# A four-layer graph network on one core: other PSUM banks and a thinned transfer queue at the head of a loop, and a pass that starts on rows that are already mixed

## The chip, the core and the metric

The kernel runs on one core of a Trainium2 chip. The core has five engines that run side by side, each with its own queue of instructions: TensorE (PE in the profile; its weight loads are listed as PEld), VectorE (DVE), ScalarE (ACT), GpSimd (POOL) and SyncE (SP). Here SP does little else than issue transfers (DMA); POOL issues the gathers (indirect transfers) and some small arithmetic. The engines meet only at semaphores. Working memory is SBUF, with 128 partitions; matmuls write to PSUM, eight banks of 512 fp32 numbers in each partition.

The metric is the device time of one execution in microseconds, as a median over runs. A profile is one further execution, with every instruction's start and length.

## What is computed

A graph of 2708 nodes with 128 features each, and a dense 2708 x 2708 adjacency `adj`, most of whose entries are zero. Four layers, each added to its input and normalized:

```python
x = layernorm(x + L0(x, adj))   # nearest-neighbour layer
x = layernorm(x + L1(x, adj))   # attention layer
x = layernorm(x + L2(x, adj))   # normalized adjacency
x = layernorm(x + L3(x, adj))   # adjacency, concatenation, relu

def L1(X, A, W, a):             # the layer that matters here
    XW = X @ W
    s_col, s_row = XW @ a[0, :128], XW @ a[0, 128:]
    den = exp(leaky_relu(s_row[:, None] + s_col[None, :], 0.01))
    num = A @ den
    att = where(num != 0, den / num, 0)
    return A @ (att @ XW)       # the last product is a pass over A
def L2(x, A, W, b):
    d = 1 / sqrt(A.sum(1) + 1e-6)
    return (d[:, None] * A * d[None, :] @ x) @ W.T + b
def L3(x, A, W, b):
    return relu(concat([x, A @ x]) @ W.T + b)
```

Everything is fp32.

## The kernel before

The adjacency comes transposed (`adjT`) and is too large to stay in SBUF: of its 22 row tiles (21 of 128 rows and one of 20) six stay in `res`, the others stream through a ring buffer, `ring`. A *pass* over the adjacency (`by_panels`, line 189) runs over six column chunks of at most 512; for each it sums 21 products of 128 rows, and for every third chunk the last 20 rows of three chunks. It makes a chunk's result in one PSUM bank (`acc`), which `into_hT` (line 231) copies out with ACT. Four panels of four row tiles each are loaded per chunk by SP (line 178), into the four slots of the ring. `by_panels` runs four times; its *third last* run is the last product of L1, `A @ (att @ XW)`, and the two after it belong to L2 and L3.

`att @ XW` is the *loop* (`block_layer`, line 1674). Nodes are sorted by score and taken in 44 blocks of 62, two blocks a step. Within a block, the sum `num` is known from running totals of the blocks before it (`carry`) and the adjacency rows of the block's own nodes. A step works on one half of the columns (HALF = 1354) and one pair of blocks q; 22 pairs by two halves give 44 steps. The 1354 columns are worked on as a *wide* piece of 1024 and a *narrow* one of 330. Step i does this:

- `load(i + 2)` (line 1119): two gathers on POOL (line 1123) bring the two blocks' adjacency rows into one of three strips of the ring, and two transfers on SP (line 1130) bring their two rows of running totals out of `carry`.
- `fetch_xw` (line 1102): POOL gathers a tile of XW rows, in the first steps.
- `find_num` (line 1683): TensorE makes `num` for the narrow piece of step i and for the wide piece of step i + 1 (line 1689).
- `add(i - 1)` (line 1708): TensorE adds the step before into `hacc` (line 1571), three banks.
- `find_inv` (line 1694): ACT makes 1/num by a logarithm and an exponential (lines 1546 and 1549).
- `mix_1`, `mix_2`, `mix_3` (lines 1556, 1560, 1563): DVE corrects and weighs it. The first of them reads `num` and makes `err`.
- `keep` (line 1697): SP stores rows of `err` as new running totals into `carry` (line 1704); usually four transfers a step.

All engines run the loop in the order in which the program writes it (`manual_schedule`); outside, a scheduler places the instructions. Tiles carry their own dependencies: whoever writes a tile or takes over its memory waits for those who used it.

The PSUM of the loop is one pool, `ops`: two buffers of two banks for the wide `num`, one bank for the narrow, three for `hacc`. Before the loop the same eight banks hold, in order, three `acc`, three `mis`, `places` and a count tile.

*Ahead of the loop* the running totals of every fourth block come from a product over the whole adjacency (`add_line`, line 1418), a row tile and a half of the columns at a time, into two `acc` banks, one for each half. `end_half(h)` (line 1435) copies such a bank to SBUF with ACT (lines 1440 and 1441), and `send_half` (line 1445) stores it in four transfers into the rows of `carry` from 96 on (line 1449): for the left half from ACT's queue, for the right half, with which TensorE ends, from SP's. Steps 0 to 21 use the left half of `carry`, steps 22 to 43 the right half. The last 20 rows of the adjacency, which the product over the adjacency needed in another arrangement, are loaded back in six transfers (line 1539). In SP's queue the scheduler puts three of these six earlier, among panel loads; the other three come last. The order there is: rows for steps 0 and 1, four stores, three reloads, the branch, rows for step 2.

*After the loop* its last `add` follows ten transposes (line 1755) of the left half's result, which ACT scales into `mixed` (line 1757), the weights of the pass that follows; `mixed` and `carry` are the same memory. Then `hacc` of the right half is copied to SBUF in three pieces (`evacuate`, lines 160 and 162). `two_layers` (line 1763) turns the other twelve tiles (line 1772), DVE scales them into `mixed` (line 1773), and the pass begins. `first` is the number of tiles mixed before, 10 (`EARLY`). For another distribution of the scores there is `dense_layer` in place of `block_layer`; it is not run here.

L253 with output `dinv` is a power on POOL for the layer after; L252 on DVE makes its input.

Of the kernel before, what the change touches and what calls it, by code (L numbers as in the profile page):

```python
# [52 lines left out]
def kernel(  # L53
# [132 lines left out]
        for g in range(1, GROUPS):  # L186
            (engine or nc.scalar.copy)(rows[few(g)], rows[few(0)])

    def by_panels(weights, done, tick=None, ready=(), first=None):

        ready = list(ready)
        accs = {}

        def product(c, i, src, w):
            lhsT = weights(i)[few(c) if i == FULL else slice(None)]
            start = c not in accs  # L200
            if start:
# [36 lines left out]
    def rows_of(y):  # L238
        return lambda i: y[:, i, :]
# [892 lines left out]
    with tc.tile_pool(name="rank", bufs=1) as rank:  # L1132
# [302 lines left out]
        def end_half(h):  # L1435

            if not carries:
                carries.append(big.tile([P, NQ * P], F32, tag="y", name="carry"))
            tot = heads[h]
            nc.scalar.copy(tot[:, : edges[4] - edges[3]], banks[h][:, : edges[4] - edges[3]])  # L1440
            nc.scalar.copy(tot[:64, edges[4] - edges[3] :], banks[h][:64, edges[4] - edges[3] : span])
            if h == 0:
                send_half(h, tot, nc.scalar)

        def send_half(h, tot, queue):

            for g in range(4):
                w = edges[g + 1] - edges[g]
                queue.dma_start(
                    carries[0][HEADS : HEADS + 2 * NCH, h * HALF + edges[g] : h * HALF + edges[g + 1]],  # L1450
                    tot[32 * g : 32 * g + 2 * NCH, :w],
                )
# [81 lines left out]
        xws, lw = work["xws"], work["lw"]  # L1534
        load(0)
        load(1)
        send_half(1, heads[1], nc.sync)
        for c in range(C):
            nc.sync.dma_start(res[few(c), FULL - S, cols[c]], adjT[FULL * P :, cols[c]])
        order.close()  # L1540
    more.close()

# [37 lines left out]
    mixed = carry.rearrange("p (t d) -> p t d", d=D)  # L1580
    EARLY = HALF // P
    over = nc.values_load(flag[0:1, 0:1], min_val=0, max_val=N)
    def dense_layer():


        nonlocal mis_pool, hT
        with (
# [6 lines left out]
            y2g = carry.rearrange("p (t d) -> p t d", d=D)  # L1594
            nc.sync.dma_start(y2g[:, :FULL, :], y2_rows[: FULL * P, :].rearrange("(t p) d -> p t d", p=P))
            nc.sync.dma_start(y2g[:LAST, FULL, :], y2_rows[FULL * P :, :])
            load_x(range(T))
            add_bias(b2_sb)

# [74 lines left out]
    def block_layer():  # L1674
        with (
            tc.tile_pool(name="own", bufs=2) as own,
            tc.tile_pool(name="ops", bufs=1, space=bass.MemoryType.PSUM) as ops,
        ):
            nc.scalar.preload_act_table_set("natural_log_exp_and_others")
            nums, invs, haccs = {}, {}, {}  # L1680
            pieces = {"wide": (0, WIDE, 2), "narrow": (WIDE, NARROW, 1)}

            def find_num(i, piece):
                q, (c0, w, bufs) = steps[i][1], pieces[piece]
# [11 lines left out]

            def keep(i, piece, err):

                (h, q), (c0, w, _) = steps[i], pieces[piece]
# [8 lines left out]
            def add(i):  # L1708
                h, q = steps[i]
                if q == 0:  # L1710
                    haccs[h] = ops.tile([P, 3 * CW], F32, tag="hacc", name="hacc")
                for piece, (c0, w, _) in pieces.items():
                    add_up(w, q, invs[i, piece], haccs[h][:, c0 : c0 + w])

            engines = {nc.tensor, nc.vector, nc.scalar, nc.sync, nc.gpsimd}
            with tc.manual_schedule(engines={e.engine for e in engines}):
# [3 lines left out]
                for i, (h, q) in enumerate(steps):  # L1720
                    if i + 2 < len(steps):
                        load(i + 2)
                    if late_q:
                        fetch_xw(xws, late_q.pop(0))
                    find_num(i, "narrow")
                    if i + 1 < len(steps):
                        find_num(i + 1, "wide")
# [8 lines left out]
                        nc.scalar.copy(mT[:, :HALF], haccs[0][:, :HALF])  # L1736
                    if i + 1 < len(steps):
                        errs = {}
                        for piece, (c0, w, _) in pieces.items():
# [4 lines left out]
                        for piece, (c0, w, _) in pieces.items():  # L1744
                            mix_3(w, q, invs[i, piece], h * HALF + c0)
                    else:
                        for piece, (c0, w, _) in pieces.items():
# [14 lines left out]

    def two_layers(arm, first):
        nonlocal acc_pool, mis_pool, hT
        acc_pool = arm.enter_context(tc.tile_pool(name="acc2", bufs=3, space=bass.MemoryType.PSUM))
        mis_pool = arm.enter_context(tc.tile_pool(name="mis2", bufs=5, space=bass.MemoryType.PSUM))

        hT = gb
        for t in range(first, T):
            p = pw[t]  # L1770
            pt = mis_tile()
            nc.tensor.transpose(pt[:p, :D], mT[:, t * P : t * P + p], ident)  # L1772
# [110 lines left out]
```

## Time and profile before

| what | us |
|---|---|
| median of 8 runs | 1039.68 |
| lowest and highest of them | 1036.59 and 1043.03 |
| the profiled execution | 1035.87 |
| its span in the trace | 1034.1 |
| head of the loop, first num matmul | 477.48 |
| the loop's last hacc matmuls end | 700.3 |
| third last pass, first product | 702.77 |

The profiled execution's mean granted clock of TensorE was 0.986. How the page goes on in time, in 40 slices of 25.9 us each; a digit is the busy share in tenths:

```profile
PE   0789999999999999798999999999999999999996
DVE  5886438999966578856999999992212121222222
ACT  0000126555611236405777776661101000020000
POOL 5000000000557763027665444410211000000000
DMA  9999340000167757696565455566675866575662
```

The run of nines in the right half of DVE's row is the loop: DVE is as full as TensorE there. After it come the three last passes, in which TensorE is full and the others mostly idle. In rows of the profile a group is given by its line and engine and by output and input (`num<-ring,lw`: from the ring and the block weights into `num`). An fp32 matmul stands in the trace as two records, so that x12 is six matmuls. SPq is SP's queue: the rows give the issuing of a transfer, not its landing.

### The profile page before, as it was taken

To read this page: it belongs to the slowest core of one execution; us is meant where nothing else is said; L and a number is where in the kernel's file an instruction comes from. 1 tells how busy PE (TensorE), PEld (TensorE's weight loads), DVE (VectorE), ACT (ScalarE), POOL (GpSimd) and SP (SyncE) were. 2 spreads that over 40 slices of the span, in tenths; PEclk is the share of its full clock that TensorE was granted. 3 is DMA by queue.
4 is the path that set the end of the run, shared out by engine and by line. 5 is a ranking of instruction groups with operands and counts; after the bars stand their busy time and mean duration, and the time that the engine had idled before them with its cause. 6 is when DMAs were issued, how large, how long until landed. Compare 5 with 4: busy or idle time off the path is not lost.

```text
span 1034.1 us, 11663 instructions
## 1 busy us (share of the span) xinstructions
PE 971.1 (94%) x3773; PEld 475.7 (46%) x3773; DVE 638.9 (62%) x1364; ACT 332.2 (32%) x609; POOL 261.5 (25%) x339
## 2 busy tenths in 40 slices
PE   0789999999999999798999999999999999999996
PEld 0346544444444557463333333344445444664444
DVE  5886438999966578856999999992212121222222
ACT  0000126555611236405777776661101000020000
POOL 5000000000557763027665444410211000000000
PEclk9899999999999999799999999999999999999998
DMA  9999340000167757696565455566675866575662
GB/s 323 374 370 315 90 160 1 0 1 1 44 218 234 234 160 253 253 399 196 147 168 148 131 150 154 137 204 208 193 224 154 289 202 215 144 261 179 205 185 62
DMA packets 101985, 191.00 MB, mean 185 GB/s; under 512 B 14006, under 2 KB 43326, under 8 KB 101914
## 3 DMA queue, kind: packets, MB, share of 16 engines
q1 hardware_dynamic: 83880, 152.34, 44.4%
q0 software_dynamic: 17728, 37.62, 13.3%
q8 instruction: 32, 0.52, 0.2%
q14 instruction: 39, 0.32, 0.1%
q10 hardware_dynamic: 306, 0.20, 0.1%
HBM read 214.80 MB, written 4.16 MB: 212 GB/s over the span
## 4 chain that ended last, share of the span: by engine, by line
PE 50%; DVE 1%; ACT 1%; DMA 0%; issue 0%; POOL 0%; POOLq 0%
PE acc L204 28%; PE hacc L1571 10%; PE num L1689 10%; PE mis L285 1%; PE mis L1818 0%; DMA ring<-carry 0%; ACT gb L234 0%; PE mis L1784 0%; DVE inv L1560 0%; PE mis L1814 0%; DVE inv L1563 0%; POOL rstd L253 0%; DVE err L1556 0%; PE mis L1772 0%; ACT m_rows L160 0%
## 5 line engine op out<-in xcount | busy, mean ns | idle before, releaser
L1123 POOL DMA_INDIRECT ring<-in_adjT,slot_i x88 | 92.9, 1056 | 95.4 <-PE num L1689 76.3
L1689 PE MATMUL num<-ring,lw 128*64 128x512 f32 (+1 forms) x528 | 111.5, 551 | 4.9 <-DMA ring<-carry 2.4
L1571 PE MATMUL hacc<-inv,xws 128*128 128x512 f32 (+1 forms) x264 | 111.7, 560 | 0.3 <-DVE inv L1563 0.3
L714 PE MATMUL acc<-zT,z 128*128 128x512 f32 (+2 forms) x252 | 102.2, 552 | 0.0
L1546 ACT ACTIVATE inv<-num,plain 128x1024 f32<-128x1024 f32 x88 | 80.6, 916 | 57.9 <-PE num L1689 43.6
L253 POOL TENSOR_TENSOR rstd<-rstd,minus_half 128x4 f32<-128x4 f32 (+1 forms) x18 | 17.3, 959 | 311.8 <-DVE rstd L252 311.8
L234 ACT COPY gb<-acc 128x512 f32<-128x512 f32 (+2 forms) x18 | 9.6, 534 | 249.4 <-PE acc L204 249.4
L715 ACT COPY key<-acc 128x512 f32<-128x512 f32 (+2 forms) x126 | 67.1, 534 | 55.1 <-PE acc L714 27.7
L1571 PEld LDWEIGHTS hacc<-inv,xws 128*128 128x128 f32 x264 | 46.6, 190 | 77.1 <-issue 32.8
L204 PE MATMUL acc<-ring,y 128*128 128x512 f32 (+2 forms) x192 | 80.4, 547 | 0.5 <-issue 0.5
L1556 DVE TENSOR_TENSOR err<-inv,num 128x1024 f32<-128x1024 f32 x88 | 74.6, 853 | 9.0 <-ACT inv L1549 6.9
L759 POOL DMA_INDIRECT got<-y_rows,where x66 | 71.2, 1079 | 30.1 <-DVE near_sum L772 10.2
L1563 DVE SCALAR_TENSOR_TENSOR inv<-gb,g_inv,inv 128x1024 f32<-128x1024 f32 x88 | 77.0, 912 | 0.1
L204 PE MATMUL acc<-ring,xs 128*128 128x512 f32 (+2 forms) x192 | 76.7, 543 | 0.0
L204 PE MATMUL acc<-ring,carry 128*128 128x512 f32 (+2 forms) x192 | 74.5, 542 | 0.0
L204 PE MATMUL acc<-ring,m_rows 128*128 128x512 f32 (+2 forms) x192 | 74.3, 542 | 0.0
L1560 DVE SCALAR_TENSOR_TENSOR inv<-err,inv 128x1024 f32<-128x1024 f32 x88 | 72.5, 861 | 0.1
L714 PEld LDWEIGHTS acc<-zT,z 128*128 128x128 f32 x252 | 45.9, 190 | 50.3 <-issue 44.9
L1549 ACT ACTIVATE inv<-inv 128x1024 f32<-128x1024 f32 x88 | 67.6, 768 | 2.8
L584 POOL TENSOR_TENSOR slot_e<-near,sim 128x44 f32<-128x44 f32 (+2 forms) x3 | 0.7, 238 | 253.9 <-DVE near L581 253.8
L1689 PEld LDWEIGHTS num<-ring,lw 128*64 128x64 f32 x528 | 35.8, 136 | 62.6 <-issue 47.6
L718 DVE MAX8 near<-key 128x8 f32<-128x2708 f32 x21 | 62.3, 2965 | 2.7 <-ACT key L715 2.7
(379 smaller groups left out, 1355.4 us busy)
## 6 DMA issues: line engine op xcount, KB each, us to landing
ring<-in_adjT SPq DMA_DIRECT2D x74, 1024.0 KB
ring<-in_adjT SPq DMA_DIRECT2D x20, 677.0 KB
ring<-in_adjT SPq DMA_DIRECT2D x17, 768.0 KB
part<-in_adjT SPq DMA_DIRECT2D x12, 1024.0 KB
ring<-in_adjT SPq DMA_DIRECT2D x17, 552.0 KB
more<-in_adjT SPq DMA_DIRECT2D x10, 677.0 KB
res<-in_adjT SPq DMA_DIRECT2D x4, 1280.0 KB
part<-in_adjT SPq DMA_DIRECT2D x3, 768.0 KB
```

The costliest lines, as they stand in the source:

```text
L204: nc.tensor.matmul(accs[c][: lhsT.shape[-1], :w], lhsT=lhsT, rhs=src, start=start, stop=stop)
L714: nc.tensor.matmul(pks[c][:p, : cw[c]], lhsT=z2[:, :p], rhs=zT[:, cs], start=False, stop=True)
L715: nc.scalar.copy(key[:p, cs], pks[c][:p, : cw[c]])
L759: nc.gpsimd.indirect_dma_start(out=got[:p, :], out_offset=None, in_=y2_rows[:, :], in_offset=bass.IndirectOffsetOnAxis(ap=where[:p, t, k : ...
L1123: nc.gpsimd.indirect_dma_start(out=rows[i][:KC, n, :], out_offset=None, in_=adj_half[:, :], in_offset=bass.IndirectOffsetOnAxis(ap=slot_i[ ...
L1546: nc.scalar.activation(inv, num[:, :w], AF.Ln, scale=plain[:, 0:1], bias=plain[:, 1:2])
L1549: nc.scalar.activation(inv, inv, AF.Exp, scale=-1.0)
L1556: nc.vector.tensor_mul(err, inv, num[:, :w])
L1560: nc.vector.scalar_tensor_tensor(inv, err, 2.0, inv, op0=ALU.subtract, op1=ALU.mult)
L1563: nc.vector.scalar_tensor_tensor(inv, gb[:, col : col + w], g_inv[:, q : q + 1], inv, op0=ALU.max, op1=ALU.mult)
L1571: nc.tensor.matmul(haccs[:, o:e], lhsT=xws[:, q, :], rhs=inv[:, o:e], start=(q == 0), stop=(q == NQ - 1))
L1689: nc.tensor.matmul(num[n * (BJ + 2) : (n + 1) * (BJ + 2), o:e], lhsT=lw[:, 2 * q + n, :], rhs=rows[i][:, n, c0 + o : c0 + e], start=True, ...
```

## The change

There are three edits.

1. In the loop, the wide `num` tiles of even and odd steps come from two pools of their own, the narrow one and `hacc` from two more. The pools are opened so that `hacc` has the banks of the three `acc` tiles, the narrow `num` that of the first `mis`, the odd steps those of the other two `mis`, and the even steps those of `places` and the count. The right half's two copies in `end_half` are made by DVE.
2. The four stores of the right half move into the loop, one in each of steps 4 to 7, and the six reloads of the last rows, one in each of steps 8 to 13. Each stands on SP behind the step's two row loads and ahead of its stores of `err`. (In the branch with `dense_layer` the reloads stand at its beginning.)
3. `by_panels` takes a function to call after a given number of products of the first chunk. The third last pass begins with eight products, then the twelve transposes and scalings come, then the rest. The two PSUM pools of the passes change places.

The diff without its renamings:

```diff
-    def by_panels(weights, done, tick=None, ready=(), first=None):
+    def by_panels(weights, done, tick=None, ready=(), first=None, between=(0, None)):
...
                 product(c, i, src, w)
+                if c == 0 and i + 1 == between[0]:
+                    between[1]()
...
             tot = heads[h]
-            nc.scalar.copy(tot[:, : edges[4] - edges[3]], banks[h][:, : edges[4] - edges[3]])
-            nc.scalar.copy(tot[:64, edges[4] - edges[3] :], banks[h][:64, edges[4] - edges[3] : span])
+            copy = nc.vector.tensor_copy if h else nc.scalar.copy
+            copy(tot[:, : edges[4] - edges[3]], banks[h][:, : edges[4] - edges[3]])
+            copy(tot[:64, edges[4] - edges[3] :], banks[h][:64, edges[4] - edges[3] : span])
...
-        def send_half(h, tot, queue):
+        def send_half(h, tot, queue, groups=range(4)):
-            for g in range(4):
+            for g in groups:
...
         load(0)
         load(1)
-        send_half(1, heads[1], nc.sync)
-        for c in range(C):
-            nc.sync.dma_start(res[few(c), FULL - S, cols[c]], adjT[FULL * P :, cols[c]])
+        right = heads[1]
...
+    def last_rows_back(chunks):
+        for c in chunks:
+            nc.sync.dma_start(res[few(c), FULL - S, cols[c]], adjT[FULL * P :, cols[c]])
...
-            tc.tile_pool(name="ops", bufs=1, space=bass.MemoryType.PSUM) as ops,
+            tc.tile_pool(name="hops", bufs=1, space=bass.MemoryType.PSUM) as hops,
+            tc.tile_pool(name="nops", bufs=1, space=bass.MemoryType.PSUM) as nops,
+            tc.tile_pool(name="odd", bufs=1, space=bass.MemoryType.PSUM) as odd,
+            tc.tile_pool(name="even", bufs=1, space=bass.MemoryType.PSUM) as even,
...
+            def num_tile(n, w, name):
+                pool = nops if w == NARROW else (even, odd)[n % 2]
+                return pool.tile([P, w], F32, tag=f"num{w}", name=name)
...
-                num = nums[i, piece] = ops.tile([P, w], F32, tag=f"num{w}", name="num", bufs=bufs)
+                num = nums[i, piece] = num_tile(i, w, "num")
...
                     if late_q:
                         fetch_xw(xws, late_q.pop(0))
+                    if 4 <= i < 8:
+                        send_half(1, right, nc.sync, (i - 4,))
+                    elif i - 8 in range(C):
+                        last_rows_back((i - 8,))
                     find_num(i, "narrow")
...
-                for t0 in range(0, EARLY, WIDE // P):
+                for n, t0 in enumerate(range(0, EARLY, WIDE // P)):
                     ts = range(t0, min(t0 + WIDE // P, EARLY))
-                    pt = ops.tile([P, WIDE], F32, tag=f"num{WIDE}", name="pt", bufs=2)
+                    pt = num_tile(len(steps) + n, WIDE, "pt")
...
+        mis_pool = arm.enter_context(tc.tile_pool(name="mis2", bufs=5, space=bass.MemoryType.PSUM))
         acc_pool = arm.enter_context(tc.tile_pool(name="acc2", bufs=3, space=bass.MemoryType.PSUM))
-        mis_pool = arm.enter_context(tc.tile_pool(name="mis2", bufs=5, space=bass.MemoryType.PSUM))
...
-        for t in range(first, T):
-            p = pw[t]
-            pt = mis_tile()
-            nc.tensor.transpose(pt[:p, :D], mT[:, t * P : t * P + p], ident)
-            nc.vector.tensor_scalar_mul(mixed[:p, t, :], pt[:p, :D], f_out[:p, t : t + 1])
-        spread(mixed[:, FULL, :])
+        def mix_rows():
+            for t in range(first, T):
+                p = pw[t]
+                pt = mis_tile()
+                nc.tensor.transpose(pt[:p, :D], mT[:, t * P : t * P + p], ident)
+                nc.vector.tensor_scalar_mul(mixed[:p, t, :], pt[:p, :D], f_out[:p, t : t + 1])
+            spread(mixed[:, FULL, :])
...
         inv_sqrt_of(dinv, deg, DEG_EPS)
+        if not first:
+            mix_rows()
...
-        by_panels(rows_of(mixed), into_hT(end_layer1))
+        by_panels(rows_of(mixed), into_hT(end_layer1), between=(first // 4 * 4, mix_rows))
```

More of the change, by code (lines that the diff above doesn't have):

```diff
@@ L1596, in dense_layer @@
             nc.sync.dma_start(y2g[:LAST, FULL, :], y2_rows[FULL * P :, :])
+            last_rows_back(range(C))
             load_x(range(T))
@@ L1680, in block_layer @@
             nums, invs, haccs = {}, {}, {}
-            pieces = {"wide": (0, WIDE, 2), "narrow": (WIDE, NARROW, 1)}
+            pieces = {"wide": (0, WIDE), "narrow": (WIDE, NARROW)}
+            def num_tile(n, w, name):
+                pool = nops if w == NARROW else (even, odd)[n % 2]
+                return pool.tile([P, w], F32, tag=f"num{w}", name=name)
             def find_num(i, piece):
-                q, (c0, w, bufs) = steps[i][1], pieces[piece]
-                num = nums[i, piece] = ops.tile([P, w], F32, tag=f"num{w}", name="num", bufs=bufs)
+                q, (c0, w) = steps[i][1], pieces[piece]
+                num = nums[i, piece] = num_tile(i, w, "num")
                 for o in range(0, w, CW):
@@ L1697, in keep @@
             def keep(i, piece, err):
-                (h, q), (c0, w, _) = steps[i], pieces[piece]
+                (h, q), (c0, w) = steps[i], pieces[piece]
                 for n in range(2):
@@ L1710, in add @@
                 if q == 0:
-                    haccs[h] = ops.tile([P, 3 * CW], F32, tag="hacc", name="hacc")
-                for piece, (c0, w, _) in pieces.items():
+                    haccs[h] = hops.tile([P, 3 * CW], F32, tag="hacc", name="hacc")
+                for piece, (c0, w) in pieces.items():
                     add_up(w, q, invs[i, piece], haccs[h][:, c0 : c0 + w])
@@ L1738, in block_layer @@
                         errs = {}
-                        for piece, (c0, w, _) in pieces.items():
+                        for piece, (c0, w) in pieces.items():
                             errs[piece] = mix_1(w, nums[i, piece], invs[i, piece], own)
@@ L1743, in block_layer @@
                             mix_2(invs[i, piece], errs[piece])
-                        for piece, (c0, w, _) in pieces.items():
+                        for piece, (c0, w) in pieces.items():
                             mix_3(w, q, invs[i, piece], h * HALF + c0)
                     else:
-                        for piece, (c0, w, _) in pieces.items():
+                        for piece, (c0, w) in pieces.items():
                             mix_2(invs[i, piece], mix_1(w, nums[i, piece], invs[i, piece], own))
                             mix_3(w, q, invs[i, piece], h * HALF + c0)
-                for t0 in range(0, EARLY, WIDE // P):
+                for n, t0 in enumerate(range(0, EARLY, WIDE // P)):
                     ts = range(t0, min(t0 + WIDE // P, EARLY))
-                    pt = ops.tile([P, WIDE], F32, tag=f"num{WIDE}", name="pt", bufs=2)
+                    pt = num_tile(len(steps) + n, WIDE, "pt")
                     for t in ts:
```

## The prediction

> **What bounds the kernel now.** I read the page's engine row first, then the chain of waits, then the two seams that the diff touches, with PE's waits and the queue of SP there.
>
> ```profile
> PE 971.1 (94%) x3773; PEld 475.7 (46%) x3773; DVE 638.9 (62%) x1364; ACT 332.2 (32%) x609; POOL 261.5 (25%) x339
> ...
> PE num L1689 <- DMA ring<-carry: 2.4, 2, 1.6
> PE num L1689 <- DVE err L1556: 1.9, 1, 1.9
> PE mis L1772 <- ACT m_rows L160: 1.9, 1, 1.9
> ```
>
> TensorE is busy 94% of the span; PE's waits (total, times, longest) show what is left. From 489.8 to 688 us the chain alternates num groups of 2.43 us and hacc groups of 2.47 us without a gap: 4.90 us a step, TensorE's own work. So the change can gain only in its gaps before and after the loop, and lose only by opening new ones. The head of the loop, on PE, SP and POOL (start, length, group, in brackets the idle time before it):
>
> ```profile
> 477.48 4.31 PE L1689 MATMUL num<-ring,lw 128*64 128x512 f32 x20 [0.66 <-ACT m_rows L1441]
> 485.25 1.04 PE L1689 MATMUL num<-ring,lw 128*64 128x512 f32 x2 [0.80 <-DMA ring<-carry]
> 487.88 1.91 PE L1689 MATMUL num<-ring,lw 128*64 128x512 f32 x6 [1.59 <-DMA ring<-carry]
> ...
> 477.41 3.18 SPq L1449 DMA_DIRECT2D carry<-m_rows  x4
> 480.63 1.26 SPq L1539 DMA_DIRECT2D res<-in_adjT  x3
> 483.07 1.42 SPq L1130 DMA_DIRECT2D ring<-carry  x2
> 484.65 2.68 SPq L1704 DMA_DIRECT2D carry<-err  x4
> ...
> 477.76 3.90 POOL L253 TENSOR_TENSOR dinv<-dinv,minus_half 128x22 f32<-128x22 f32 x1
> 483.27 1.06 POOL L1123 DMA_INDIRECT ring<-in_adjT,slot_i  x1 [0.30 <-issue]
> 485.10 1.75 DVE L1563 SCALAR_TENSOR_TENSOR inv<-gb,g_inv,inv 128x1024 f32<-128x1024 f32 x2
> ```
>
> The rows that step 2 needs (L1130, issued 483.07) stand on SP behind seven transfers of the right half, and the second pair's row is the 3.85 us piece in the chain:
>
> ```profile
> 483.90 3.85 DMA ring<-carry
> ...
> 489.79 2.47 PE hacc L1571 x6
> ...
> 700.34 0.59 ACT m_rows L160
> 700.96 0.70 DVE m_rows L162
> 701.69 0.44 ACT m_rows L160
> 702.17 0.77 PE mis L1772 x5
> ```
>
> The last four are the other seam: TensorE ends its last hacc group at 700.3 and idles until three copies are through, 1.87 us.
>
> **The change, part by part.**
>
> *A. First num in other banks.* Before, its banks were those that ACT was still copying out at L1440 and L1441, hence the 0.66 us. In the built order of the changed kernel the first num matmul waits only for its two loads (rows issued at 467.1, gathers at 467.4 and 468.8, needed nine us later). TensorE can go on from 476.8: -0.66 us. Bounds: -0.85 (it follows the last matmul's issue) and 0 (another wait stands there).
>
> *B. Seven transfers off SP's head.* Step 2's row transfers now come right after steps 0 and 1's; they wait only for the berths' last matmul, near 474, so even a latency of 4.7 us has them there by 479. The 2.4 us of DMA wait go. What is late next is DVE: the first hacc group needs inv, whose wide mix at L1563 starts at 485.10 and takes about 1.25 (1.75 for the wide and narrow pair, of which a narrow one alone takes 0.56): 486.35. Before, the group began at 489.79, so 489.79 - 486.35 = 3.4 us, and DVE's whole chain (err 481.98, waiting for ACT, that for num) moves with A. A and B: -4.1. The 1.88 us for err stay, since the narrow num still has one buffer.
> DVE's pace allows it: from err at 481.98 to the next err at 486.77 is 4.79 us for a step, against TensorE's 4.90, so the lead, nil at the first hacc group, grows by 0.1 us a step.
>
> *C. What is late after that.* Steps 3 and 4 are then wanted 4 us earlier, and their gathers are not: POOL is held by L253 to 481.66, and its gathers follow each other at its own pace. L253 may start 0.35 later, as its input L252 now stands on DVE behind the two copies moved there (0.44 and 0.15 on ACT; 0.69 is DVE's row for 128x512), which wait for 476.8. Step 3's rows follow step 0's four err transfers: err ends near 482.5, 4 x 0.67 gives 485.1, two more 486.4. Landing after 2 to 4.7 us (by the trace's landing records the head's SP transfers took 2.0 to 4.7, those behind gathers the longer) they are there at 487.7 to 490.5; wanted at 485.7 + 2.47 + 0.65 = 488.8. Step 4's: wanted at 493.7, there at 492.5 to 495. I take 0.3 us of wait in all, near the transfer that landed with the gather before it, at 488.8; bounds 0 and 2.0. Before, 0.26 was lost there too (a 2.69 us num piece where 2.43 is normal), so +0.1 net, rounded up.
> On this the Trainium skill speaks (DMA: Bandwidth & Descriptors, section "Anatomy of one DMA — SWDGE (gpsimd) path"): a small transfer costs a fixed 2.0 us or so, nearly all completion. By that the rows would land at 488 and C would cost nothing, 0.3 us less in the sum; the 3.85 us row shows that behind gathers it does not hold here, so the row decides.
>
> *D. One transfer more a step, steps 4 to 13, on SP.* Between a step's two row loads and its err transfers SP is idle: rows end at 512.94, err begins at 514.04, 1.1 us. A right-half store takes 3.18 / 4 = 0.80 us, a reload 1.26 / 3 = 0.42. They fit: 0. If that cover is gone (early steps spaced at 0.67, 6 x 0.67 + 0.80 = 4.8 of 4.9 us) they delay the err rows and the next loads by tenths, against some 2 us between landing and use in a settled step: still 0. The carry's right half is read first at step 20. The three reloads that stood earlier on SP (0.32 us each near 374 us, among panel loads that wait for TensorE) free nothing. ACT loses the two copies, DVE gains them at a time when it idles 5.59 us.
>
> *E. Third last pass starts with mixed rows.* Eight products (0.86 us each) now stand before the twelve transposes. They need rows 0 to 7, which ACT has scaled by 700.0, and the first panels, landed long ago, since SP issued them from 684 on. The first product waits for ACT and for a bank whose last reader is that scaling. So TensorE goes from 700.3 on; the 1.87 us of idle go, and the copies lie under 6.9 us of products. Transposes and scalings keep their length (DVE 12 x 0.28 = 3.4 us, row 10 wanted 3 us after the first transposes). Bounds: -2.0 (the full 700.15 to 702.17) and -1.0 (a drain and a semaphore twice). I take -1.85. The pools' swapped order moves banks only.
>
> **Sum.** -4.1 + 0.1 + 0 - 1.85 = -5.85 us. The profiled execution took 1035.87 us (span 1034.1 and 1.8 around it): 1030.0. It lies 3.8 under the median of the runs shown, 1039.68; the median would go to **1033.8 us**.
>
> **Rivals.**
> *R1, the wait moves to step 3.* Removing the wait at step 2 only bares the next loads: gathers held by the 3.90 us on POOL, rows behind them. For it: two gathers follow each other at 1.4 us on POOL, and landings up to 4.7 us. Against: both land by about 488.3 in step 3. At worst 2.0 us come back: 1039.68 - 3.85 = 1035.8.
> *R2, a seam stays shut.* The new first product or the new first num waits for something that the profile hasn't shown, such as TensorE's own drain before reusing a bank. For it: the built order gives that product waits for TensorE and ACT. E's loss to its bound 1.0 and A's to 0: 1039.68 - 4.3 = 1035.4. Were the whole change not to do what it says, 1039.7.
> *R3, slower: SP runs out of transfers in flight.* In the built order each SP transfer waits for the one eight before it to land. With seven a step, eight landings of mean L set a step of 7L/8; TensorE's 4.90 is passed at L = 5.6 us. At L = 6.6 a step takes 5.8, and ten steps lose 9 us against the 5.85 gained: 1042.8. It decides from 0.6 us a step (L = 6.3). For it: gathers took 4.5 us and over. Against: SP's own landings in the loop lie at 2 to 4.7.
>
> **How the numbers follow.** Forecast 0.68, R1 0.14, R2 0.09 (0.04 of it no change at all), R3 0.05; 0.04 for something else, half without effect, half slower. I take 0.2% (2.1 us) as what a measurement of this kernel can tell from no change. The forecast, R1 and most of R2 are faster: 0.87 after a little is taken off for scatter; same 0.07; slower 0.06. The forecast's own range is A to E's bounds, gains of 4.5 to 6.6, and about 1.5 us by which a median of runs that spread from 1036.6 to 1043.0 can shift: 1031.5 to 1036.5. With R1 and R2, 1031.2 to 1037.2.
>
> **What would show it.** Right: no wait of num for the last copy, SP's rows for step 2 issued before 476 us, the first hacc group near 485.7, waits for ring<-carry under 0.6 us in all, no PE idle before the first product, the transposes near 707 less the shift, and the loop still 4.90 a step. Wrong: PE waits for DMA at wide num of steps 3 and 4 above 1 us (R1), an idle time over 0.8 us before the first product (R2), steps 4 to 13 longer than 4.90 (R3), or DVE waits at hacc of over 0.2 us after the third step.

## The result and the profile after

The changed kernel takes 1034.74 us (median of 24 runs, 1032.52 to 1039.04); the kernel before, run beside it, 1039.68 (66 runs). The ratio is 0.9951, 95% interval 0.9939 to 0.9964: 4.9 us faster, where 5.85 was forecast. The profiled execution has a span of 1033.2 us.

Two executions are best compared from one event on, the end of the last line matmul ahead of the loop (476.82 us before, 478.32 after). The seam is the time from the start of the loop's last hacc group to the copy of the first chunk of the third last pass.

| us | before | after |
|---|---|---|
| last line matmul to first num | 0.66 | -0.07 |
| last line matmul to first hacc group | 12.89 | 8.84 |
| what the next 42 steps lose over their normal length | 0.26 | 2.4 |
| the seam | 25.11 | 23.04 |
| last line matmul to the copy of the first chunk | 246.06 | 242.12 |

The page's row of busy times, and the timeline of PE at the head (start, length, group, in brackets the idle time before it and what ended it):

```profile
PE 974.0 (94%) x3773; PEld 475.9 (46%) x3773; DVE 638.8 (62%) x1366; ACT 331.6 (32%) x607; POOL 265.9 (26%) x339
```

```profile
478.25 4.22 PE L1704 MATMUL num<-ring,lw 128*64 128x512 f32 x20
484.33 2.50 PE L1704 MATMUL num<-ring,lw 128*64 128x330 f32 x12 [1.86 <-DVE err L1557]
487.17 2.51 PE L1572 MATMUL hacc<-inv,xws 128*128 128x512 f32 x6 [0.34 <-ACT inv L1550]
489.61 2.99 PE L1704 MATMUL num<-ring,lw 128*64 128x330 f32 x12
492.52 2.54 PE L1572 MATMUL hacc<-inv,xws 128*128 128x512 f32 x6
494.99 2.99 PE L1704 MATMUL num<-ring,lw 128*64 128x330 f32 x12
497.90 2.54 PE L1572 MATMUL hacc<-inv,xws 128*128 128x512 f32 x6
...
519.99 0.78 PE L1704 MATMUL num<-ring,lw 128*64 128x330 f32 x4
521.59 2.33 PE L1704 MATMUL num<-ring,lw 128*64 128x512 f32 x8 [0.83 <-DMA ring<-carry]
523.85 2.54 PE L1572 MATMUL hacc<-inv,xws 128*128 128x512 f32 x6
```

The 0.66 us ahead of the first num are gone, and so are the 0.80 and 1.59 us in which TensorE waited for step 2's rows. Two things are new. Two num groups take 2.99 us where 2.50 is normal: a group in which matmuls wait singly for the wide pieces of steps 3 and 4. By the trace's landing records the last to land was in both the second block's row, sent by SP (490.55 and 495.94 us), 0.2 us behind that block's gather on POOL (490.32 and 495.76). And before the wide num of step 9 TensorE waits 0.83 us, for the first block's row on SP, and then takes 2.33 for eight records, since the second block's gather lands at 521.94; so this step is 1.43 us too long.

The rows of SP (its queue; issuing, not landing) and of POOL:

```profile
472.19 3.73 SPq L1132 DMA_DIRECT2D ring<-carry  x3
...
515.16 1.23 SPq L1132 DMA_DIRECT2D ring<-carry  x2
516.45 0.81 SPq L1452 DMA_DIRECT2D carry<-m_rows  x1
517.35 2.69 SPq L1719 DMA_DIRECT2D carry<-err  x4
```

```profile
479.48 3.88 POOL L255 TENSOR_TENSOR dinv<-dinv,minus_half 128x22 f32<-128x22 f32 x1 [0.23 <-DVE dinv L254]
483.57 1.10 POOL L1125 DMA_INDIRECT ring<-in_adjT,slot_i  x1 [0.22 <-issue]
...
507.71 1.04 POOL L1125 DMA_INDIRECT ring<-in_adjT,slot_i  x1 [0.30 <-issue]
509.06 1.47 POOL L1125 DMA_INDIRECT ring<-in_adjT,slot_i  x1 [0.30 <-issue]
510.83 1.33 POOL L1105 DMA_INDIRECT xws<-xw_rows,row_j  x1 [0.30 <-issue]
512.47 1.04 POOL L1125 DMA_INDIRECT ring<-in_adjT,slot_i  x1 [0.30 <-issue]
```

Step 2's rows are now issued before 476 us. A store (L1452) stands in the gap between the row loads and the err transfers. POOL's brackets are to be read closely: ahead of every transfer an idle time of 0.30 us, the least that its rows show between two transfers, up to 526 us. POOL is behind all that time. The same timeline of the kernel before, one settled step:

```profile
513.10 1.04 POOL L1123 DMA_INDIRECT ring<-in_adjT,slot_i  x1 [0.98 <-PE num L1689]
514.45 1.05 POOL L1123 DMA_INDIRECT ring<-in_adjT,slot_i  x1 [0.30 <-issue]
515.80 1.22 POOL L1103 DMA_INDIRECT xws<-xw_rows,row_j  x1 [0.30 <-issue]
```

There POOL waits 0.98 us in each step until TensorE has left the strip: POOL is ahead. The chain of waits of the changed kernel at the other seam:

```profile
697.40 2.54 PE hacc L1572 x6
699.94 6.88 PE acc L204 x16
706.82 0.55 PE mis L1793 x5
```

The first eight products follow the last hacc group with no idle time, the transposes come behind them.

Up to the first chunk's copy 3.94 us are gained, yet the profiled spans differ by only 0.9. The rest is the clock. In windows of both kernels (length, busy time of PE, PEld, DVE, ACT and POOL with counts, then PEclk, the granted clock), first before, then after:

```profile
400.00:440.00 40.00, 33.21 (x335) 22.46 (x333) 34.09 (x100) 24.11 (x44) 4.26 (x7) 0.83 0.76 272
...
930.00:945.00 15.00, 15.00 (x55) 7.58 (x54) 6.00 (x28) 2.09 (x7) 1.01 (x1) 1.00 0.22 70
```

```profile
400.00:440.00 40.00, 33.53 (x326) 22.32 (x324) 33.81 (x99) 23.84 (x43) 3.63 (x6) 0.79 0.71 254
...
930.00:945.00 15.00, 15.00 (x46) 7.51 (x46) 5.70 (x26) 1.55 (x5) 1.01 (x1) 0.89 0.13 36
```

0.04 of 40 us and 0.11 of 15 us are 3.2 us at full clock, the 3.0 us missing. Neither stretch holds code that the change touches, and in other executions of the changed kernel the low clock lies elsewhere, so this is no effect of the change; it is why medians of many runs are compared here, and parts of a profile rather than whole spans.

### The profile page after: what moved, and what is told of

The parts are those of the page before. It is cut to its first block, busy times and chain, and to the rows that moved or that the text cites. A ratio compares the mean times of both kernels' runs of the same rounds, so it can differ in the third digit from the quotient of the medians.

```text
span 1033.2 us, 11663 instructions
## 1 busy us (share of the span) xinstructions
PE 974.0 (94%) x3773; PEld 475.9 (46%) x3773; DVE 638.8 (62%) x1366; ACT 331.6 (32%) x607; POOL 265.9 (26%) x339
## 4 chain that ended last, share of the span: by engine, by line
PE 83%; DVE 7%; DMA 5%; ACT 2%; issue 1%; POOL 0%; SPq 0%; POOLq 0%; DVEq 0%; ACTq 0%
PE acc L204 33%; PE hacc L1572 10%; PE num L1704 9%; PE acc L430 9%; PE acc L716 8%; PE acc L1422 3%; DMA res<-in_adjT 3%; PE acc L706 2%; DMA got<-y_rows,where 1%; PE mis L287 1%; DVE near L720 1%; DVE both L506 1%; DVE where L730 1%; PE mis L1147 1%; DMA ring<-carry 1%
## 5 line engine op out<-in xcount | busy, mean ns | idle before, releaser
L1125 POOL DMA_INDIRECT ring<-in_adjT,slot_i x88 | 96.5, 1097 | 88.8 <-PE num L1704 68.0
L255 POOL TENSOR_TENSOR rstd<-rstd,minus_half 128x4 f32<-128x4 f32 (+1 forms) x18 | 17.3, 959 | 311.3 <-DVE rstd L254 311.3
```

Source lines behind the costliest of these rows:

```text
L1125: nc.gpsimd.indirect_dma_start(out=rows[i][:KC, n, :], out_offset=None, in_=adj_half[:, :], in_offset=bass.IndirectOffsetOnAxis(ap=slot_i[ ...
```

## The experiments

In the order in which they ran. The chips differ, so each time stands beside the kernel before on the same chip: 1060.36 us (35 runs) for the first four, 1057.23 for the next four, 1040.68 for the last four. Each experiment has 12 runs. These scatter over some 10 us, so the differences of profiles from the last line matmul on carry more than the times.

### The three edits one by one

The changed kernel once more, as it is.

> The changed kernel once more, for its profile. In its first profile it gained 4.1 us from the last line matmul to the first hacc group, gave back 0.2, 0.5 and 1.4 us at the wide nums of steps 3, 4 and 9 and won 2.1 us at the pass. Theory T1 (step 9's wait comes from the stores of steps 4 to 7 in a stretch whose gathers already move most): it is there again, 1.0 to 1.8 us at the same step. Theory T2 (chance: how the transfers happened to fall): it is gone or elsewhere. Both: the head again 4.1 us, the pass 2.1 us, time 4 to 6 us under the kernel before.

1058.53 us, ratio 0.9976 (0.9953 to 0.9999): 1.8 us under the kernel before, not 4 to 6. First hacc group 9.26 us after the last line matmul, seam 23.04. The steps lost 0.42 and 1.30 at steps 3 and 4 and 2.20 at step 9: the same three places, more on this chip. Of the 2.20 only 0.9 are at the wide num, a little under T1's 1.0 to 1.8; the other 1.3 are a wait of hacc for ACT, which is taken up at the second edit. That the wide nums wait at these steps is no accident of one execution; what makes it was open.

The third edit alone, with the banks and the queue of before:

```diff
+ between=(first // 4 * 4, mix_rows), mis2 ahead of acc2
- hops, nops, odd, even; stores and reloads in the loop
```

> The third edit alone: eight products ahead of the twelve transposes, head and loop as before. By the prediction 1.85 us less than before (2.1 by the changed kernel's profile), all of it between the last hacc group and the first product. If the idle time only moved (the first product waits for its bank and for the engine's drain) it gains under 1 us.

1060.19 us, ratio 0.9993 (0.9970 to 1.0015): nothing. PE's waits (total, times, longest) and the chain of waits say why:

```profile
PE acc L204 <- ACT m_rows L160: 1.9, 1, 1.9
```

```profile
720.38 2.55 PE hacc L1575 x6
722.95 0.59 ACT m_rows L160
723.57 0.70 DVE m_rows L162
724.78 8.83 PE acc L204 x16
```

The transposes' wait of before has gone over to the first product, with the same 1.87 us: it waits for the copies out of hacc (L160, L162). So the edit's order is not enough; which condition was missing is taken up below (pass_banks). (8.83 in place of 6.88 us is a stretch of half clock, as the granted clock there shows.)

The second edit alone:

```diff
+ if 4 <= i < 8: send_half(1, right, nc.sync, (i - 4,))
+ elif i - 8 in range(C): last_rows_back((i - 8,))
  (one pool ops, ACT's copies and the pass of before)
```

> The second edit alone: stores and reloads out of the head, one a step in steps 4 to 13; banks, copies and pass as before. By the prediction 3.4 us less up to the first hacc group, of which 0.7 to 2.1 come back at the wide nums of the early steps: 1.3 to 2.7 us less in time. T1: a wait of about a microsecond near step 9. Rival: without the first edit nothing is gained, since the first num's wait for the copies sets the head.

1057.0 us, ratio 0.9973 (0.9947 to 0.9998). The first hacc group came at 9.69 instead of 12.89: 3.2 us, where B's share was worked out at 3.4. Then the steps lost 5.8 us, of which about 1.7 are a stretch of half clock near 562 us. The largest wait is of another kind:

```profile
560.93 3.65 PE L1572 MATMUL hacc<-inv,xws 128*128 128x512 f32 x6 [2.07 <-ACT xws L1749]
```

```profile
558.29 1.20 ACT L1547 ACTIVATE inv<-num,plain 128x1024 f32<-128x1024 f32 x1 [3.79 <-PE num L1700]
560.49 0.39 ACT L1749 ACTIVATE xws<-xws,g_col 128x128 f32<-128x128 f32 x1
```

TensorE waited until ACT had scaled a tile of xws. No transfer made this wait: POOL issued the gather of that tile at 521.96 us, and it landed at 525.48, 35 us before ACT scaled it. ACT was late because the wide logarithm ahead of it in its queue had waited 3.79 us for TensorE, although the num that it reads ends at 553.97 in PE's rows. The trace has no semaphore update of TensorE between 553.34 and 558.23 us, and then six within 0.22 us; why, no run shows. The 1.3 us at hacc in changed_again, and the 1.9 us in changed_third below, come with a like gap and burst in TensorE's updates, and their tiles had landed 34 us before. So these waits are neither POOL's nor SP's, and they are kept apart from the waits at the wide nums from here on. In this profile the wide nums of steps 3, 4, 8 and 9 lost 0.67, 0.31, 0.49 and 0.57, 2.0 us in all, within the 0.7 to 2.1 expected.

The first edit alone:

```diff
+ hops, nops, odd, even; the right half's copies on DVE
  (stores and reloads at the head, the pass of before)
```

> The first edit alone: other banks for num, the right half's copies on DVE, stores and reloads at the head of SP's queue as before. The first num begins 0.7 us earlier, but step 2's rows still stand behind seven transfers that wait for the same copies; so the first hacc group begins where it did, and the time is the same within 0.4 us. Rival: the 0.7 us go through to the end.

1060.06 us, ratio 1.0005 (0.9982 to 1.0027). The first num starts at -0.07 and the first hacc group at 12.18 instead of 12.89: the 0.7 us went through, with the wait for step 2's rows still there (1.6 us in this profile). The time doesn't resolve it. At the seam the transposes wait 0.7 instead of 1.9 us, and the seam is 24.50 instead of 25.11, so that 0.6 of its gain come from the banks alone:

```profile
PE mis L1791 <- ACT m_rows L160: 0.7, 1, 0.7
```

### What makes the waits of steps 3, 4 and 9

Two theories. S: the stores and reloads among the gathers lengthen their landing. P: the 3.88 us power on POOL (L255) makes POOL late, and it cannot catch up. Four kernels on one chip.

> The changed kernel once more, as it is, to stand beside the three below. In its profiles so far the steps after the first hacc group lost 0.45 + 0.48 + 1.43 = 2.4 us over 4.90 each (first profile) and 0.42 + 1.30 + 2.20 = 3.9 (second). Both theories expect 2 to 4 us there again, and POOL with only 0.30 us before each transfer until about step 10.

1054.07 us, ratio 0.9964 (0.9939 to 0.9989). The steps lost 1.40 and 1.17 at steps 3 and 4 and 2.11 at step 9, 4.7 in all. But at step 9 the wide num lost only 0.2; the rest is hacc's wait for ACT:

```profile
PE hacc L1572 <- ACT xws L1753: 1.8, 1, 1.8
```

So the wide nums lost 2.8.

```diff
-                    if 4 <= i < 8:
-                        send_half(1, right, nc.sync, (i - 4,))
-                    elif i - 8 in range(C):
-                        last_rows_back((i - 8,))
+                    if 14 <= i < 18:
+                        send_half(1, right, nc.sync, (i - 14,))
+                    elif i - 24 in range(C):
+                        last_rows_back((i - 24,))
```

> The changed kernel with the right half's stores in steps 14 to 17 and the reloads in steps 24 to 29. Theory S (the stores and reloads among the gathers lengthen their landing, 7.2 and 8.1 us against 5.9 and 6.1 before, and so make the wait for step 9's load): that wait goes, what stays are the 0.4 to 1.3 us at steps 3 and 4, and the time falls 1.4 to 2.2 us under the changed kernel's. Theory P (the 3.88 us power on POOL at the loop's head is never made up, since three transfers of a step take POOL 4.75 of TensorE's 4.90 us): the waits stay, the time is within 0.5 us of the changed kernel's.

1054.19 us, ratio 0.9974 (0.9948 to 1.0000). Losses 1.30, 1.08 and 1.21, all at the wide nums: 3.6. PE's timeline has all three places still:

```profile
504.14 1.63 PE L1704 MATMUL num<-ring,lw 128*64 128x330 f32 x6
506.04 1.93 PE L1704 MATMUL num<-ring,lw 128*64 128x512 f32 x6 [0.27 <-issue]
...
510.37 3.57 PE L1704 MATMUL num<-ring,lw 128*64 128x330 f32 x12
...
535.92 3.71 PE L1704 MATMUL num<-ring,lw 128*64 128x330 f32 x12
```

The wide num of step 9 lost 1.2 us, where the changed kernel beside it lost 0.2. With the stores and reloads away the waits stay; theory S as the whole cause falls, and no gain of this edit is seen.

```diff
+                    if i + 3 == len(steps):
+                        inv_sqrt_of(dinv, deg, DEG_EPS)
                     find_num(i, "narrow")
...
-        inv_sqrt_of(dinv, deg, DEG_EPS)
         if not first:
+            inv_sqrt_of(dinv, deg, DEG_EPS)
             mix_rows()
```

> The changed kernel with the addition and power of dinv (DVE and 3.88 us of POOL) taken from the loop's head to behind the loop's last load, near step 41. Theory P: POOL waits for TensorE again from step 3 or 4 on, as in the kernel before (about 1 us ahead of each load), the gathers of steps 3, 4 and 9 leave 3 us sooner, the steps' losses fall from 2.4 to 3.9 us to under 0.6, and the time is 2 to 3 us under the changed kernel's. Theory S: steps 3 and 4 gain at most 0.9 us, the wait for step 9's load stays at 1.4 to 2.2. If the power at its new place held something up, POOL's row near 690 us would show a wait of TensorE behind it; none is expected, as dinv is read only after the loop.

1051.88 us, ratio 0.9963 (0.9941 to 0.9986); the median is 2.2 us under the changed kernel's beside it, the ratios are alike. The loss is 1.1 us at step 3, nothing at steps 4 and 9: 1.1 where the wide nums of the changed kernel lost 2.8, but more than the 0.6 expected. POOL's timeline:

```profile
504.45 1.33 POOL L1125 DMA_INDIRECT ring<-in_adjT,slot_i  x1 [1.03 <-PE num L1704]
...
509.73 2.02 POOL L1125 DMA_INDIRECT ring<-in_adjT,slot_i  x1 [0.93 <-PE num L1704]
...
525.55 1.04 POOL L1125 DMA_INDIRECT ring<-in_adjT,slot_i  x1 [0.75 <-PE num L1704]
```

POOL waits for TensorE again, from the first steps on, as theory P says. What stays at step 3 has another cause:

```profile
509.93 2.37 PE L1704 MATMUL num<-ring,lw 128*64 128x512 f32 x8 [0.49 <-DMA ring<-carry]
```

The two gathers of step 3 had landed at 504.10 and 505.35 us, 4 us ahead of need; its two rows on SP, which stand behind the err stores of step 0, landed at 509.79 and 510.25. Both edits together:

> Both edits together. Theory P: as power_late alone, within 0.5 us. Theory S: the steps' losses go only here, 2.4 to 3.9 us under the changed kernel. If each takes its own part, this is the fastest of the four and the two single gains add up.

1052.13 us, ratio 0.9943 (0.9920 to 0.9965). Losses 0.32 at step 3 and 0.23 at step 9. That is 0.6 us less than with the power alone, in one profile each; with the stores alone the wide nums had lost more than in the changed kernel, so the single gains don't add up.

### Three checks

The power moved in the kernel before:

> The kernel before, with the addition and power of dinv moved behind the loop's last load, as in power_late. Theory P says that TensorE's wait for step 2's rows covered the 3.9 us of POOL there: POOL waits for TensorE ahead of every load in the kernel before, so the move changes nothing (within 1 us), the first hacc group stays some 12.9 us behind the last line matmul, and the steps stay at 4.90 us but for the first. If the power cost time by itself, in either kernel, this one would gain 2 us or more as power_late did in its profile.

1039.4 us, ratio 0.9994 (0.9971 to 1.0017), 1.3 us in medians and no difference that the interval tells from none. The profile shows why little can come of it:

```profile
495.53 1.04 POOL L1123 DMA_INDIRECT ring<-in_adjT,slot_i  x1 [5.20 <-PE num L1689]
```

POOL just waits longer, 5.20 us, for TensorE. (The first hacc group came at 13.61, with a stretch of half clock near 486 us in it.) In the kernel before the wait for step 2's rows covered the power; the change took the cover away.

The first and third edit without the second:

```diff
  (the changed kernel)
+ send_half(1, right, nc.sync) and six reloads at the head
- stores and reloads in the loop
```

> The changed kernel with the right half's seven transfers back at the loop's head: the banks and the third last pass's start together. The pass's edit alone left TensorE waiting 1.87 us ahead of its first product, for ACT's copy out of hacc. If that was the layout of the banks, which the first edit makes, the seam is 23.04 us here as in the changed kernel, and the head gains 0.7 at most: 2 to 2.7 us under the kernel before. If the first product waits for something else, the seam stays at 24.5 to 25.1 and the gain at 0.7 or less.

1039.38 us, ratio 0.9986 (0.9962 to 1.0011). The time is inconclusive: 6.8 us of half clock lie in the profiled head too, where the first hacc group came at 14.59. The seam is not; the chain of waits:

```profile
699.73 2.54 PE hacc L1575 x6
702.27 6.88 PE acc L204 x16
709.15 0.55 PE mis L1791 x5
```

23.04 us, no idle time. So the third edit needs the first one's order of banks: without it the first product's bank is one that the copies out of hacc still read. By the order in which the pools are opened, it is the third edit's own exchange of the two pools that puts `acc` there; the third edit without this exchange, in the banks of before, was not run.

Last, the changed kernel beside the one with both later:

> The changed kernel as it is, beside the next. Theory P: POOL has only 0.30 us ahead of its transfers for some ten steps, and the steps lose 2.4 to 4.7 us over 4.90 each, as in the three profiles of it so far.

1036.36 us, ratio 0.9955 (0.9930 to 0.9980). POOL was behind from step 3 on, and stayed so until its xws gathers ran out near 555 us, but the losses were 0.36 and 0.36, and step 9 waited for nothing: the expected 2.4 to 4.7 was missed. Being late on POOL uses up the margin; whether a wait comes of it depends on how long the transfers take in that execution. The gathers of step 9 left POOL as late as in the first profile and took 5.7 and 6.0 us here (7.2 and 8.1 there), its rows 4.8 and 4.4 (6.3 and 5.9).

> The changed kernel with the power behind the last load and the stores and reloads in steps 14 to 17 and 24 to 29, once more. In its first profile the steps lost 0.5 us. Theory P with a smaller share for the stores: 0.5 to 1.5 us here, and the time 2 to 4 us under the changed kernel's beside it; if its lead was scatter, the two are within 1 us.

1033.84 us, ratio 0.9940 (0.9915 to 0.9965). A loss of 0.49 at the first hacc group is a stretch of half clock (3.4 us from 484.3), not a wait. At step 9 0.61 are lost, although POOL waited for TensorE all along: the gathers had landed at 519.55 us, the rows landed last, at 519.93 and 520.11. In medians 2.5 us under the changed kernel, 1.9 in the pair before; in both pairs the intervals overlap. It has the lowest ratio of each set of four, but these runs don't fix by how much it is faster.

What the wide nums lost, in one table (us over the normal num group; "late" means that POOL has only its 0.30 us ahead of its transfers; hacc's waits for ACT and half clock left out):

| kernel | POOL | step 3 | step 4 | step 9 |
|---|---|---|---|---|
| changed, four profiles | late | 0.5, 0.4, 1.4, 0.4 | 0.5, 1.3, 1.2, 0.4 | 1.4, 0.9, 0.2, 0.0 |
| second edit alone | late | 0.7 | 0.3 | 0.6 |
| stores later | late | 1.3 | 1.1 | 1.2 |
| power late | waits for PE | 1.1 | 0.0 | 0.0 |
| both, two profiles | waits for PE | 0.3, 0.0 | 0.0, 0.0 | 0.2, 0.6 |
| first edit alone, third edit alone | waits for PE | 0.4, 1.0 | 0.0, 0.0 | 0.5, 0.6 |

Step 4 is settled: all six profiles with POOL late lose there, none of the others does. In the first profile of the changed kernel and in changed_fourth it was a row on SP that landed last there, but with POOL in time the rows too land sooner after their issue: 2.4 and 2.0 us in power_late, 2.2 and 2.0 in both_again, against 3.9 and 4.1 in the first profile and 4.3 and 3.8 in changed_fourth. Steps 3 and 9 are not settled: they lose with POOL in time as well. The loss at step 3 with POOL in time is a wait for rows on SP. At step 9 transfers take long in the kernel before too (its gathers 5.9 and 6.1 us, where those of steps 5 to 8 took 3.3 to 5.6), and its rows land only 0.85 and 1.05 us ahead of need; what makes them longer still in some executions stays open.

## Why the prediction was right, and where not

**A, the banks, -0.66.** Right: -0.73, carried on to the first hacc group (banks_alone, 0.7).

**B, the queue; A and B -4.1.** Right in mechanism and size: 12.89 to 8.84 is 4.05. The first hacc group waits 0.34 us, for inv, as the step said: DVE and ACT's chain set it, no longer rows on SP. Alone it gave 3.2 of 3.4.

**C, what is late next, +0.1 net.** This term was mis-sized: +2.1 in the first profile (2.4 lost against 0.26), 0.4 in the mildest of four. 0.93 were lost at steps 3 and 4, where the step had 0.3, and 1.43 at step 9, which it didn't look at. For steps 3 and 4 it named both transfers that came late, the gathers held by the power and the rows behind the err stores, and they landed within 0.2 us of each other; it sized the two losses some tenths too small. It followed POOL to step 4 only, on the unspoken assumption that POOL then has time to catch up. It doesn't. A settled step of the kernel before has 0.98 us of waiting on POOL; in the changed kernel POOL's step is 507.71 to 512.47, 4.76 us, with no waiting in it, so of TensorE's 4.90 only 0.14 are left to make up 3.9. What was measured on single transfers (1.04 and 1.05 for the gathers, 1.22 for xws) became 1.04, 1.47 and 1.33. In changed_fourth, from the load for step 13 on, POOL's step was 4.90 and the second gather took 1.66: nothing was left at all.

For step 9 the working then runs so. Before, its two gathers left POOL 36.3 us after the last line matmul (513.10), after 34.2 (512.47): 2.1 us sooner, while TensorE came 3.3 sooner. By the trace's landing records they took 5.9 and 6.1 us before and 7.2 and 8.1 after; the two rows on SP 4.8 and 4.3 before, 6.3 and 5.9 after. All had landed at 521.57 before, 521.94 after. TensorE took up the wide num at 522.42 before, 3.07 us behind the start of the hacc group ahead of it, so 0.85 us after the last landing; by the same distance it would have been ready at 520.58 after. The first block began at 521.59, behind its row (521.45), the second at 521.98, behind its gather (521.94): 1.4 us late. Of the 3.3 us by which this gather fell behind TensorE, 1.2 are POOL's lateness and 2.1 its longer landing. The rule of the Trainium skill that the prediction set against C (DMA: Bandwidth & Descriptors, "Anatomy of one DMA — SWDGE (gpsimd) path") is stated there for transfers of GpSimd's queue: a fixed 2.0 us or so and the bytes at 436 GB/s. For a gather of 62 rows of 5.4 KB that is an estimate of 2.8 us; those of step 9 took 5.9 to 8.1, so it doesn't hold among these gathers. The prediction applied it to rows that SP sends, of which that section does not speak; they took 2.0 to 6.3 us.

**D, one more transfer a step on SP, 0.** Not shown to be wrong, but its cover was thinner than it said. The gap of 1.1 us on SP is used up (rows are issued at 510.36 and again at 515.16, with no gap over 0.1 us between SP's seven transfers: 4.8 us, as the step reckoned for its bad case). The "some 2 us between landing and use" were 0.85 and 1.05 at step 9 of the kernel before. With the stores and reloads moved away the wide num of step 9 lost no less (1.2 us against 0.2, one profile each), and the timed medians of the two, 1054.19 and 1054.07, show no difference.

**E, the third last pass, -1.85.** Right: -2.07 (25.11 to 23.04), a little past its bound of -2.0. "The pools' swapped order moves banks only" hid a condition: with the banks of before the third edit closes nothing (pass_alone), with the first edit's it closes all (pass_banks). The bank "whose last reader is that scaling" is there only with the first edit, since the exchange of the pools moves `acc`.

**The sum.** -4.05 + 2.1 - 2.07 = -4.0 to the first chunk's copy in the first profile; the median fell by 4.9. The forecast of -5.85 is about what the mildest profile of the changed kernel has (240.43 to the first chunk's copy against 246.06: -5.6); in the other three it is -3.9, -2.0 and -1.7. In the three later comparisons the changed kernel's ratio was 0.9976, 0.9964 and 0.9955, nowhere a larger gain than 0.9951. So the mechanism of A, B and E was right and C's size wrong; that the median still came out 0.9 us from the forecast is in part luck, since what C costs differs by some 2 us from one execution to the next. The forecast's least gain of 4.5 leaves out C's own bound of 2.0, which went to R1.

**The rivals.** R1 came partly: the wait moved on, to steps 3 and 4 and to step 9, and its 2.0 us were reached in the first profile and passed at the wide nums in two others (2.6 and 2.8). R2 did not come; pass_alone shows what it would have been. R3, SP out of transfers in flight, did not come: the landings of its rows passed 5.6 us only at steps 9 and 10 of the first profile, and the steps there kept to 4.90 but for one.

## What to carry to other kernels

A wait that is removed was covering work on other queues. For each engine that feeds the loop, compare its own step, back to back, with the bounding engine's step: if little is left over, a lateness of a few us at the loop's head lasts for ten steps or more and shows wherever a transfer is slow. Work that nobody needs before the loop's end can stand behind it. Where several transfers feed one instruction, ask of each when it landed: an early gather gains nothing while a row on another queue lands last. And follow a wait back to its start before it is given to a cause: the wait for a scaled tile of xws had nothing to do with the gather of that tile, which had landed 35 us before. And an edit that reorders work at a seam is worth only what the layout of memory lets it be: look for who still reads the bank.

## What was not expected of the hardware

POOL's transfers get longer when it runs without waiting, and its step then has DVE's length. DVE's timeline of the changed kernel:

```profile
507.97 1.63 DVE L1561 SCALAR_TENSOR_TENSOR inv<-err,inv 128x1024 f32<-128x1024 f32 x2
...
512.73 1.63 DVE L1561 SCALAR_TENSOR_TENSOR inv<-err,inv 128x1024 f32<-128x1024 f32 x2
```

512.73 - 507.97 is 4.76 us, the same as POOL's 512.47 - 507.71. In the kernel before POOL's issue times are TensorE's, and the second gather takes 1.05 us instead of 1.47. In changed_fourth DVE's step later grows to 4.90 us, TensorE's, and that of POOL, still late, grows with it to 4.90, its second gather to 1.66. The Trainium skill (SBUF — State Buffer, "SBUF: two separate sides") states that DVE and GpSimd share a pair of ports by an exclusive lock, which a DVE instruction with two inputs in SBUF holds against a GpSimd operation that reads SBUF; a POOL that advances at DVE's pace would fit this. No run here tested it.

TensorE's clock was granted at half for some 3.4 us or a multiple of it. Some of these stretches all 14 profiles have (near 40 us, between 414 and 450 and in the last 10 us), others differ from one execution to the next (near 486, 504, 562, 725 or 936 us, among other places); each 3.4 us costs 1.7. TensorE's idle time doesn't explain the one at 936: in the window from 930 to 945 us shown above PE is busy for all of 15.00 us. Over the 83 runs of the last comparison a run was 0.9 us longer for each 0.001 less in its mean granted clock (a straight line through all, one level for each kernel): so a large part of the scatter of 10 us goes with the clock.
